# Which groups of a graph convolution are multiplied by an adjacency and which are gathered: 20 and 5, or 15 and 10, with a recorded engine order

## Chip, cores and metric

The kernel runs on one core of one Trainium2 chip. The metric is the device time of one execution in microseconds, as the median of several runs.

## The reference

Four layers, each a graph convolution and a feed-forward part, run over 3125 nodes of 256 features and 53125 edges, sorted by destination; each node has one edge to itself in that list. The change touches the third graph part (L2) and the building of what it multiplies with. Cut to what matters:

```python
def _L2_gnn_ref(x, W1, b1, W2, b2, edge_index):
    loops = jnp.arange(n)
    src = concatenate([edge_index[0], loops])      # the loops come on top of the
    dst = concatenate([edge_index[1], loops])      # own edges already in the list
    deg = segment_sum(ones, dst); dinv = rsqrt(deg)
    norm = dinv[src] * dinv[dst]
    def gcn_conv(h, W, b):
        m = (h @ W)[src] * norm[:, None]
        return segment_sum(m, dst) + b
    x1 = gcn_conv(x, W1, b1)
    x1 = x1 / max(norm_of_row(x1), 1e-12)
    x2 = gcn_conv(x1, W2, b2)
    return x2 + x

x = x + _L1_gnn_ref(...); x = x + _L1_ffn_ref(layernorm(x), ...)
x = x + _L2_gnn_ref(layernorm(x), W1, b1, W2, b2, edge_index)
x = x + _L2_ffn_ref(layernorm(x), ...)             # a switch layer; its router comes first
```

All else (the other three graph parts and feed-forward parts) is the same in both kernels.

## The kernel before

**Groups and slots.** The nodes are ranked by degree and cut into `NT` = 25 groups of 128. Group g has `KS[g]` slots, as many as its node with the most edges has: 41, 25, 23, 22, 21, 21, 20, 20, 19, 19, 18, 18, 17, 17, 16, 16, 16, 15, 15, 14, 14, 13, 12, 11, 10. `BATCH` = 5 groups share the small operations. A node lies on a partition, its features along the free axis.

**A convolution** (`edge_sum`) starts from `own`, the rows h @ W times dinv, in SBUF, and from the same rows in a table in HBM. The groups below `GD` = 20 are sums by matrix products: `products(g)` loads `adj[g]`, 0 and 1 in bf16, 128 x 3200 and 800 KB (tile `adj_g`, three buffers), and multiplies its 25 blocks with the rows. So that bf16 loses nothing, the rows are split into three bf16 parts (`F12`, in the buffer of `XNT`, and `F3_`); per block there is one matmul of 512 columns (L2851) and one of 256 (L2854). Two additions put the halves together with `own` (`sum`, L2871 and L2872). The groups from `GD` on are gathered: each slot is an indirect DMA of 128 rows, issued by POOL (`gt<-gcn,z_i`, issued in the helper at L1082), four slots to a tile `gt` of three buffers (`C4` = 4), and DVE sums a tile's slots and adds them to `own` (`g_part`, L2840 and L2841). One tile is taken beside each product (`next(beside)`). The own edge counts twice, once by the list and once by the loop.

**The order of groups** is written out: 0 to 14 by product, then 20 to 24 gathered, then 15 to 19 by product.

**Tails.** After a group's sum, `tail1` of the first convolution scales it, adds the bias and sums its squares; after each batch of five the rows are normalised, transposed by PE, copied by ACT and multiplied by the second weights (`to_table`, L2884), and a batch's rows go to the second table. `tail2` of the second convolution adds the residual; after each batch come the layer norm (`XN`, L2931), PE transposes (L1632), an ACT copy (L1633), the router matmul (L2937) and the logits `lgs` (L2938). The next stage begins with `bests`, the maximum over all logits. The tails are generators, so that a step of them follows each later group.

**Order on the engines.** Each engine takes its instructions in one order. What the program text gives is taken by a scheduler, which puts ready work of each engine first by its own costs, except inside `tc.manual_schedule(engines=...)`, where the named engines keep the order of the text. DMA issues lie on SP's queue, indirect DMAs on POOL's.

**The adjacencies** are built earlier, beside the gates of the L1 feed-forward part, one group to a step (`beside_gates`): `one_hots` (L2051, DVE) makes `em_p` and `em_b` for the edges of group g, `edge_blocks` multiplies them (`em_ps`, L2066, PE) and ACT copies the counts to `em_a` (L2073, L2077), which SP stores to `adj[g]`. `edge_columns` and `edge_places` prepare the slots of these groups.

Of the kernel before, what the change touches and what calls it, by code (L numbers as in the profile page):

```python
# [11 lines left out]
F32 = mybir.dt.float32  # L12
# [3 lines left out]
ALU = mybir.AluOpType  # L16
# [4 lines left out]
P = 128  # L21
D = 256
KD = D // P
N = 3125
NT = (N + P - 1) // P
# [16 lines left out]
def parts(tc, a, k, X, XNT):  # L42
# [387 lines left out]

    def moe(E, F, gates, w1, b1, w2, b2):

        FC = F // P
        with tc.tile_pool(name="mw", bufs=2) as mw, tc.tile_pool(name="mc", bufs=1) as mc:
# [5 lines left out]
            with tc.tile_pool(name="mps", bufs=3, space=PSUM) as mps, tc.tile_pool(name="mh", bufs=2) as mh:  # L440
# [4 lines left out]
                for e in range(E):  # L445
                    w1_sb = mw.tile([P, KD, F], F32, name="w1_sb")
                    nc.sync.dma_start(w1_sb, w1[e].rearrange("(k p) f -> p k f", p=P))
# [581 lines left out]
C4 = 4  # L1029


def profile():


    mean = (E - N) / N
    p = [math.exp(-mean)]
    for i in range(1, 200):
        p.append(p[-1] * mean / i)
    ks = []
    for g in range(NT):  # L1040
        d = 1
        while True:
            tail = max(1.0 - sum(p[:d]), 0.0)
            c = N * tail
            if (c < 1e-3) if g == 0 else (c + 4.0 * math.sqrt(c * (1.0 - tail)) <= P * g):
                break
            d += 1
        ks.append(d)
    return ks


KS = profile()
# [1 line left out]
TOT = sum(KS)  # L1054
DC = KS[0] + 3

GD = 20
BATCH = 5


# [20 lines left out]
def gather(nc, out_, table, idx):  # L1081
    return nc.gpsimd.indirect_dma_start(out=out_, out_offset=None, in_=table, in_offset=index(idx))  # L1082
# [509 lines left out]
def quick(ctx: ExitStack, tc: tile.TileContext, a: dict, out: bass.AP, k):  # L1592
# [3 lines left out]
    nc, dram, ident, ident_b, ones = tc.nc, k.dram, k.ident, k.ident_b, k.ones  # L1596
# [22 lines left out]
    def table_of(name, width, rows=NP + 1):  # L1619

        t = dram.tile([rows, width], F32, name=name)
        nc.sync.dma_start(t[NP : NP + 1, :], zero[:, :width])
        return t

    def batches():
        return [range(b, b + BATCH) for b in range(0, NT, BATCH)]
# [175 lines left out]
    def chunks(g):  # L1802
        return [(c, min(C4, KS[g] - c)) for c in range(0, KS[g], C4)]
# [157 lines left out]

    adj = dram.tile([GD, P, NT * P], BF16, name="adj")


    TILES, at = [], 0
    for g in range(GD):
        w = min(10, P // KS[g])
        n = -(-P // w)
# [4 lines left out]
    TB = -(-at // P)  # L1973
    slots_d = dram.tile([2 * P * OFF[GD]], F32, name="slots_d")

    def slots_of(g):
        return slots_d[2 * P * OFF[g] : 2 * P * OFF[g + 1]]

    t_at = q.tile([P, GD], F32, name="t_at")
    with tc.tile_pool(name="ep", bufs=1) as pool:  # L1980
        NJ = max(n for _, n, _ in TILES)
        firsts = pool.tile([P, GD, NJ], F32, name="ep_first")
        for g, (w, _, _) in enumerate(TILES):
# [3 lines left out]
        nc.gpsimd.iota(j_f, pattern=[[0, 1]], base=0, channel_multiplier=1, allow_small_or_imprecise_dtypes=True)  # L1987
        past = pool.tile([P, GD, NJ], F32, name="ep_past")
        nc.vector.tensor_scalar(past, firsts, j_f, None, op0=ALU.is_le)
# [687 lines left out]
    def beside_gates(pool, wp, psum):  # L2677


        EX, F = 4, 512  # L2680
        FC = F // P
        b1_sb = wp.tile([P, EX, FC], F32, name="x_b1")
# [4 lines left out]
        def load(e):  # L2687
            w1 = pool.tile([P, KD, F], F32, name="x_w1")
            nc.sync.dma_start(w1, a["L1_ffn_W1"][e].rearrange("(k p) f -> p k f", p=P))
            w2 = pool.tile([P, FC, D], F32, name="x_w2")  # L2690
            nc.sync.dma_start(w2, a["L1_ffn_W2"][e].rearrange("(f p) d -> p f d", p=P))
            b2 = pool.tile([P, D], F32, name="x_b2")
            nc.sync.dma_start(b2, a["L1_ffn_b2"][e : e + 1, :].to_broadcast([P, D]))
            ws[e] = w1, w2, b2
# [78 lines left out]
    with tc.tile_pool(name="ge", bufs=1) as gc, tc.tile_pool(name="gy", bufs=4) as gp:  # L2773
        gates = gc.tile([P, NT, C], F32, name="gates")
        nc.sync.dma_start(gates, gd.rearrange("(p t) w -> p t w", p=P))
        for g in range(NT):
            y = gp.tile([P, 4, D], F32, name="y")
            nc.sync.dma_start(y, each_d[:, g * P : (g + 1) * P, :].rearrange("e p d -> p e d"))
            for e in range(4):
                nc.vector.scalar_tensor_tensor(X[:, g, :], y[:, e, :], gates[:, g, e : e + 1], X[:, g, :],  # L2780
                                               op0=ALU.mult, op1=ALU.add)
# [14 lines left out]
    with tc.tile_pool(name="ng", bufs=3) as gp, tc.tile_pool(name="ns", bufs=3) as sp, \  # L2796
# [3 lines left out]
        own = wp.tile([P, NT, D], F32, name="own")  # L2800
# [6 lines left out]
        tables = [table_of(f"gcn{i}", D) for i in (1, 2)]  # L2807
# [8 lines left out]
        F12 = XNT.rearrange("p k n -> p (k n)").bitcast(BF16).rearrange("p (b s d) -> p b s d", s=2, d=D)  # L2816
        F3_ = wp.tile([P, NT, D], BF16, name="F3")

        def edge_sum(table, tail):


            for gs in batches():
                b = slice(gs[0], gs[-1] + 1)
                F = sp.tile([P, BATCH, D], F32, name="F", bufs=2)
                nc.scalar.copy(F12[:, b, 0, :], own[:, b, :])
                nc.vector.tensor_sub(F, own[:, b, :], F12[:, b, 0, :])
                nc.scalar.copy(F12[:, b, 1, :], F)
                nc.vector.tensor_sub(F3_[:, b, :], F, F12[:, b, 1, :])
            tails, ready = [], set()

            def gathered():

                for g in range(GD, NT):
                    for c, n in chunks(g):
                        t = gp.tile([P, C4, D], F32, name="gt", bufs=3)
                        for i in range(n):
                            k_ = OFF[g] - OFF[GD] + c + i
                            gather(nc, t[:, i, :], table, zi[:, k_ : k_ + 1])
                        part = sp.tile([P, D], F32, name="g_part", bufs=2)
                        nc.vector.tensor_reduce(part, t[:, :n, :].rearrange("p s d -> p d s"), AX.X, ALU.add)  # L2840
                        nc.vector.tensor_add(own[:, g, :], own[:, g, :], part)  # L2841
                        if c + n == KS[g]:
                            ready.add(g)
                        yield 0

            def products(g):
                A = gp.tile([P, NT, P], BF16, name="adj_g")
                nc.sync.dma_start(A.rearrange("p b j -> p (b j)"), adj[g])
                acc = psum.tile([P, 2, D], F32, name="acc", bufs=2)
                for b in range(NT):  # L2850
                    nc.tensor.matmul(acc.rearrange("p s d -> p (s d)"), A[:, b, :],  # L2851
                                     F12[:, b, :, :].rearrange("p s d -> p (s d)"),
                                     start=(b == 0), stop=False, skip_group_check=True)
                    nc.tensor.matmul(acc[:, 0, :], A[:, b, :], F3_[:, b, :], start=False, stop=(b == NT - 1),  # L2854
                                     skip_group_check=True)
                return acc

            beside = gathered()
            for g in [*range(GD - BATCH), *range(GD, NT), *range(GD - BATCH, GD)]:
                if g < GD:  # L2860
                    acc = products(g)
                    next(beside, None)
                while g >= GD and g not in ready:
                    next(beside)
                for t in list(tails):
                    if next(t, None) is None:
                        tails.remove(t)
                s_ = own[:, g, :]
                if g < GD:
                    s_ = sp.tile([P, D], F32, name="sum", bufs=2)  # L2870
                    nc.vector.tensor_add(s_, acc[:, 0, :], own[:, g, :])  # L2871
                    nc.vector.tensor_add(s_, s_, acc[:, 1, :])  # L2872
                t = tail(g, s_)
                if t:
                    tails.append(t)
            for t in tails:
                for _ in t:
                    pass
# [37 lines left out]
            yield 0  # L2916

        st = SimpleNamespace()
        edge_sum(tables[0], tail1)

        def tail2(g, acc):
            nc.vector.tensor_add(X[:, g, :], X[:, g, :], b2)
# [3 lines left out]
            if g % BATCH == BATCH - 1:  # L2926
# [3 lines left out]
                for i, g_ in enumerate(gs):  # L2930
# [8 lines left out]
                    if i % 2:  # L2939
                        yield 0  # L2940
                nc.sync.dma_start(sw_xn[gs[0] * P : (gs[-1] + 1) * P, :].rearrange("(t p) d -> p t d", p=P),
                                  XN[:, gs[0] : gs[-1] + 1, :])

        edge_sum(tables[1], tail2)


    with tc.tile_pool(name="wc", bufs=1) as wc, tc.tile_pool(name="ww", bufs=6) as ww, \
# [82 lines left out]
    with tc.tile_pool(name="ag", bufs=abufs) as gp, tc.tile_pool(name="am", bufs=2) as mp, \  # L3030
# [28 lines left out]
        for o in range(0, TOT, 160):  # L3059
            n = min(160, TOT - o)  # L3060
# [321 lines left out]
```

## Time and profile before

| | |
|---|---|
| median of 6 runs | 5787.91 us (5776.34 to 5796.77) |
| the profiled execution | 5784.42 us, its span 5782.7 us |
| mean granted TensorE clock | 0.753 |
| busy: PE, DVE, ACT, POOL | 3383.1, 3113.0, 1217.1, 2833.4 us |
| L2 convolutions: first gather, second one's first gather, `bests` | 3817.4, 4073.2, 4311.8 us from the span's start |
| gathers in them | 3817.4 to 3869.3 (39), 3879.0 to 3905.2 (21); 4073.2 to 4122.4 (39), 4132.5 to 4159 (21) |
| first and last `sum` of each | 3838.9 and 4053.1; 4083.6 and 4298.5 us |

The span is that of one execution taken by the hardware profiler. "Busy" is the time in which an engine works on an instruction; idle time is put down to what ended it, a DMA, another engine's result, or "issue", where the profile shows nothing that the engine waited for. PEld are weight loads, which may overlap the matmuls. A group of instructions is named by its line, its engine, its operation and its tiles, then the count, the busy time and the mean of one in ns. Line numbers of helpers (L1082, L1632) stand for all their callers, so that the tiles tell the stages apart.

### The profile page before, as it was taken

Reading aid. Unit: us, or ns where it says so; the run is one execution under the profiler, and the core shown is the slowest. Engines: PE = TensorE matmul, PEld = TensorE weight load, DVE = VectorE, ACT = ScalarE, POOL = GpSimd, SP = SyncE. Lnnn points to the kernel's source line nnn. Section 1 sums busy time; section 2 is a strip of 40 time slices with the busy share of each in tenths; the row PEclk is TensorE's granted clock in tenths of the full one; section 3 lists DMA queues with packets and bytes.
Section 4 is the critical chain, followed back from the end, with each engine's and each line's share of the span. In section 5 each row is a group of like instructions: output and inputs, shape, how many; then the busy total and the mean of one; then the engine's idle time right before and its main releaser. Section 6 shows DMA issues by size and latency. Waiting matters only on the chain. (4 is left out here: it accounts for less than half of the span.)

```text
span 5782.7 us, 44145 instructions
## 1 busy us (share of the span) xinstructions
PE 3383.1 (59%) x13157; PEld 2313.3 (40%) x13157; DVE 3113.0 (54%) x6119; ACT 1217.1 (21%) x3115; POOL 2833.4 (49%) x3011
## 2 busy tenths in 40 slices
PE   4245554355487964445337565059679355556995
PEld 3234443233354533334124343036354233334885
DVE  5377887798685754561124331463441567886002
ACT  1222323455531200000113231121112101111221
POOL 1567673577765036676644445430403466661223
PEclk7677777677798976676568777579885677787998
DMA  3534442334321233332212221353324333332664
GB/s 104 132 101 114 110 124 79 81 100 113 99 29 48 113 94 92 88 89 76 28 43 70 51 63 24 82 144 102 120 79 123 95 87 93 94 89 73 195 195 153
DMA packets 321843, 548.13 MB, mean 95 GB/s; under 512 B 100906, under 2 KB 224028, under 8 KB 318254
## 3 DMA queue, kind: packets, MB, share of 16 engines
q0 software_dynamic: 121840, 290.47, 20.7%
q1 hardware_dynamic: 186757, 244.81, 13.1%
q10 hardware_dynamic: 12982, 9.77, 0.6%
q8 instruction: 112, 1.84, 0.1%
q14 instruction: 152, 1.25, 0.1%
HBM read 429.05 MB, written 118.80 MB: 95 GB/s over the span
## 5 line engine op out<-in xcount | busy, mean ns | idle before, releaser
L1082 POOL DMA_INDIRECT gt<-T,recs x856 | 907.4, 1060 | 443.0 <-issue 344.7
L1841 PE MATMUL acc<-wv,ident 128*128 128x256 f32 x1812 | 557.6, 462 | 285.9 <-issue 153.0
L1082 POOL DMA_INDIRECT gt<-rel,relz x428 | 414.1, 968 | 433.2 <-issue 368.3
L1082 POOL DMA_INDIRECT gt<-gm,recs x428 | 405.6, 948 | 403.1 <-issue 200.3
L1841 PEld LDWEIGHTS acc<-wv,ident 128*128 128x128 f32 x1812 | 412.7, 235 | 408.2 <-issue 174.0
L1082 POOL DMA_INDIRECT gt<-TA,recs x428 | 436.9, 1021 | 254.8 <-issue 125.9
L1841 PE MATMUL acc<-gt,wv 128*128 128x256 f32 x906 | 296.0, 486 | 310.3 <-DVE wv L1852 256.0
L2851 PE MATMUL acc<-XNT,adj_g 128*128 128x512 bf16 x1000 | 347.4, 394 | 50.7 <-issue 39.6
L2702 PE MATMUL x_ps<-XNT,x_w 128*128 128x512 f32 (+1 forms) x448 | 244.7, 679 | 222.6 <-ACT x_h L2704 138.8
L1954 PE MATMUL acc<-gt,ident 128*128 128x256 f32 x856 | 281.4, 467 | 145.3 <-issue 121.1
L1841 PEld LDWEIGHTS acc<-gt,wv 128*128 128x128 f32 x906 | 210.3, 243 | 389.7 <-DVE wv L1852 194.4
L2723 DVE TENSOR_TENSOR x_y<-x_o,x_b 128x512 f32<-128x512 f32 (+1 forms) x52 | 34.4, 670 | 612.9 <-remote 245.4
L1914 ACT ACTIVATE m<-m 128x1024 f32<-128x1024 f32 (+3 forms) x246 | 243.1, 988 | 492.6 <-DVE m L1911 306.8
L1911 DVE TENSOR_TENSOR m<-gt,R 128x1040 f32<-128x1040 f32 (+6 forms) x246 | 281.5, 1144 | 93.8 <-DMA gt<-T,recs 54.5
L2854 PE MATMUL acc<-F,adj_g 128*128 128x256 bf16 x1000 | 280.7, 281 | 36.7 <-issue 28.4
L1919 DVE TENSOR_TENSOR m<-m,fixed 128x1040 f32<-128x1040 f32 (+6 forms) x246 | 280.2, 1139 | 36.3 <-ACT m L1914 27.1
L1954 PEld LDWEIGHTS acc<-gt,ident 128*128 128x128 f32 x856 | 193.0, 233 | 220.6 <-issue 152.6
L1082 POOL DMA_INDIRECT gt<-gcn,z_i x120 | 117.2, 977 | 320.6 <-DMA gcn<-own 168.0
L2716 PE MATMUL x_o<-x_w,x_h 128*128 128x256 f32 x800 | 208.2, 404 | 48.4 <-issue 48.1
L2702 PEld LDWEIGHTS x_ps<-XNT,x_w 128*128 128x128 f32 x448 | 92.5, 232 | 317.3 <-issue 167.7
L3142 PE MATMUL e_ps<-EW,att 128*128 128x512 bf16 (+4 forms) x233 | 94.5, 481 | 191.7 <-ACT att L3125 73.6
L3273 PE MATMUL fh_ps<-xt,w 128*128 128x256 f32 x896 | 200.0, 382 | 0.8 <-DVE xt L3265 0.8
(665 smaller groups left out, 7162.9 us busy)
## 6 DMA issues: line engine op xcount, KB each, us to landing
w<-in_L_ffn_W_dram SPq DMA_DIRECT2D x56, 1024.0 KB
adj_g<-adj SPq DMA_DIRECT2D x40, 800.0 KB
rel<-hx SPq DMA_DIRECT2D x25, 1024.0 KB
adj<-em_a SPq DMA_DIRECT2D x20, 800.0 KB
gt<-T,recs POOLq DMA_INDIRECT x856
y<-each_d SPq DMA_DIRECT2D x25, 512.0 KB
each_d<-x_y SPq DMA_DIRECT2D x24, 512.0 KB
gt<-rel,relz POOLq DMA_INDIRECT x428
```

The lines of the kernel that those rows point to most:

```text
L1082: return nc.gpsimd.indirect_dma_start(out=out_, out_offset=None, in_=table, in_offset=index(idx))
L1841: nc.tensor.matmul(acc, w, v, start=(c + s == 0 and bias is None), stop=(c + s == K - 1))
L1911: nc.vector.tensor_add(m[:, :n, :], st[g].tiles[c][:, :n, :W], st[g].R[1][:, None, :].to_broadcast([P, n, W]))
L1914: nc.scalar.activation(v, v, AF.Abs)
L1919: nc.vector.tensor_mul(m[:, :n, :], m[:, :n, :], att_row[:, None, :].to_broadcast([P, n, W]))
L1954: nc.tensor.matmul(accs[g], ident, t[:, s, :], start=False, stop=(last and s == n - 1))
L2702: nc.tensor.matmul(ps[:, :n], ws[e][0][:, c, f_ * P : (f_ + 1) * P], XNT[:, c, c0 : c0 + n], start=(c == 0), stop=(c == KD - 1))
L2716: nc.tensor.matmul(ps[:, j, :], ht[:, f_, (i + j) * P : (i + j + 1) * P], ws[e][1][:, f_, :], start=(f_ == 0), stop=(f_ == FC - 1))
L2851: nc.tensor.matmul(acc.rearrange("p s d -> p (s d)"), A[:, b, :], F12[:, b, :, :].rearrange("p s d -> p (s d)"), start=(b == 0), stop=Fals ...
L2854: nc.tensor.matmul(acc[:, 0, :], A[:, b, :], F3_[:, b, :], start=False, stop=(b == NT - 1), skip_group_check=True)
L3142: nc.tensor.matmul(e_ps[:, :z, :].rearrange("p s d -> p (s d)"), att, EW[: att.shape[0], s : s + z, :].rearrange("p s d -> p (s d)"), star ...
L3273: nc.tensor.matmul(ps[:, i, :], ld[j][1][:, c, (f_ + i) * P : (f_ + i + 1) * P], xt[j][:, c, :], start=(c == 0), stop=(c == KD - 1))
```

## The change

`GD` falls from 20 to 15: groups 15 to 19 are gathered too, so that five adjacencies fewer are built, stored and loaded, and each convolution has 15 products. The own edge is no longer gathered: the chunks cover `KS[g]` - 1 slots, and the first addition of a group takes 2 times `own`. A convolution has 126 gathers in 36 tiles (60 in 17 before). Two tiles are taken beside each of the first ten products and three beside each of the last five. The groups go 0 to 9 by product, 15 to 19 gathered, 10 to 14 by product, 20 to 24 gathered. The splitting into bf16 parts is staggered by one batch, and both calls of `edge_sum` record the order of PE, ACT and DVE. POOL and SP are still ordered by the scheduler.

```diff
-GD = 20
+GD = 15
 BATCH = 5
...
         def edge_sum(table, tail):
-            for gs in batches():
-                b = slice(gs[0], gs[-1] + 1)
-                F = sp.tile([P, BATCH, D], F32, name="F", bufs=2)
-                nc.scalar.copy(F12[:, b, 0, :], own[:, b, :])
-                nc.vector.tensor_sub(F, own[:, b, :], F12[:, b, 0, :])
-                nc.scalar.copy(F12[:, b, 1, :], F)
-                nc.vector.tensor_sub(F3_[:, b, :], F, F12[:, b, 1, :])
+            bs = [slice(gs[0], gs[-1] + 1) for gs in batches()]
+            Fs = []
+            for i in range(len(bs) + 1):
+                if i < len(bs):
+                    F = sp.tile([P, BATCH, D], F32, name="F", bufs=2)
+                    nc.scalar.copy(F12[:, bs[i], 0, :], own[:, bs[i], :])
+                    nc.vector.tensor_sub(F, own[:, bs[i], :], F12[:, bs[i], 0, :])
+                    Fs.append(F)
+                if i:
+                    nc.scalar.copy(F12[:, bs[i - 1], 1, :], Fs[i - 1])
+                    nc.vector.tensor_sub(F3_[:, bs[i - 1], :], Fs[i - 1], F12[:, bs[i - 1], 1, :])
...
                 for g in range(GD, NT):
-                    for c, n in chunks(g):
+                    for c in range(0, KS[g] - 1, C4):
+                        n = min(C4, KS[g] - 1 - c)
                         t = gp.tile([P, C4, D], F32, name="gt", bufs=3)
...
-                        nc.vector.tensor_add(own[:, g, :], own[:, g, :], part)
-                        if c + n == KS[g]:
+                        nc.vector.scalar_tensor_tensor(own[:, g, :], own[:, g, :], 2.0 if c == 0 else 1.0, part,
+                                                       op0=ALU.mult, op1=ALU.add)
+                        if c + n == KS[g] - 1:
                             ready.add(g)
...
             beside = gathered()
-            for g in [*range(GD - BATCH), *range(GD, NT), *range(GD - BATCH, GD)]:
+            early = NT - BATCH
+            for g in [*range(GD - BATCH), *range(GD, early), *range(GD - BATCH, GD), *range(early, NT)]:
                 if g < GD:
                     acc = products(g)
-                    next(beside, None)
+                    for _ in range(2 if g < GD - BATCH else 3):
+                        next(beside, None)
...
-        edge_sum(tables[0], tail1)
+        ET = mybir.EngineType
+        with tc.manual_schedule(engines={ET.PE, ET.Activation, ET.DVE}):
+            edge_sum(tables[0], tail1)
...
-        edge_sum(tables[1], tail2)
+        with tc.manual_schedule(engines={ET.PE, ET.Activation, ET.DVE}):
+            edge_sum(tables[1], tail2)
```

## The prediction

> **What bounds the kernel now.** I read the page first, for the groups of the graph convolution, then the lines view and the busy time by windows of that stage, then the timeline of one stretch, and last the lines view of the gate stage, where the adjacencies are built. The page's rows:
>
> ```profile
> L2851 PE MATMUL acc<-XNT,adj_g 128*128 128x512 bf16 x1000 | 347.4, 394 | 50.7 <-issue 39.6
> ...
> L2854 PE MATMUL acc<-F,adj_g 128*128 128x256 bf16 x1000 | 280.7, 281 | 36.7 <-issue 28.4
> ...
> L1082 POOL DMA_INDIRECT gt<-gcn,z_i x120 | 117.2, 977 | 320.6 <-DMA gcn<-own 168.0
> ```
>
> Both convolutions lie between 3817.4 us (first gather) and 4311.8 us (`bests`): 255.8 us to the second one's first gather at 4073.2, then 238.6, together 494.4. The sums of the products (L2871) leave the rhythm of the stage: every 9.2 us once no gather runs, which is 8.1 us for the 25 pairs of matmuls and about 1.05 us for one node's table or router work. PE looks like the bound. The windows say more; their columns are busy us (and instructions) of PE, weight loads, DVE, ACT and POOL, the granted clock, the DMA share and GB/s:
>
> ```profile
> 3820.00:3900.00 80.00, 42.80 (x204) 21.35 (x202) 39.10 (x57) 1.26 (x1) 52.74 (x55) 0.77 0.46 130
> 3980.00:4060.00 80.00, 79.35 (x474) 51.21 (x472) 36.03 (x88) 19.82 (x39) 0.00 (x0) 1.00 0.31 105
> 4080.00:4160.00 80.00, 40.01 (x178) 18.64 (x175) 38.47 (x55) 0.00 (x0) 52.84 (x55) 0.70 0.46 132
> 4160.00:4240.00 80.00, 78.19 (x480) 48.18 (x481) 28.46 (x93) 3.44 (x11) 0.00 (x0) 0.96 0.33 111
> ```
>
> While POOL gathers, PE gets through 204 and 178 matmuls in 80 us; without gathers, 474 and 480. The timeline shows that this is not a wait for data (start, duration, idle time before and its releaser):
>
> ```profile
> 3858.33 0.95 POOL L1082 DMA_INDIRECT gt<-gcn,z_i  x1 [0.30 <-issue]
> 3859.11 0.11 PEld L2854 LDWEIGHTS <-adj_g 128*128 128x128 bf16 x1 [2.71 <-issue]
> 3859.58 0.95 POOL L1082 DMA_INDIRECT gt<-gcn,z_i  x1 [0.30 <-issue]
> 3859.81 0.37 PE L2854 MATMUL acc<-F,adj_g 128*128 128x256 bf16 x1 [1.52 <-issue]
> 3860.84 0.95 POOL L1082 DMA_INDIRECT gt<-gcn,z_i  x1 [0.30 <-issue]
> 3861.21 0.10 PEld L2851 LDWEIGHTS <-adj_g 128*128 128x128 bf16 x1 [2.00 <-issue]
> ```
>
> PE takes one instruction in 0.7 to 1.4 us, with "issue" before it, while POOL issues a gather every 1.25 us (0.95 and 0.30). This starved state begins some 15 us after PE and POOL have both been busy, and ends 2 to 4 us after POOL stops. In the first convolution it fills 3847 to 3871 and 3892.5 to 3908.7, in the second 4100 to 4126 and 4147 to 4162: 81 us in all, 0.54 of the 120 x 1.255 = 151 us of gathering. That is the row on which everything turns, since the change doubles the gathers.
>
> The stage now closes as a sum, to 2 us. First convolution: 13.4 (first gather to first product) + 20 x 8.1 + 20 x 1.05 + 40 starved + 20.1 (last sum at 4053.1 to the next gather) = 257 against 255.8. Second: 2.3 + 162 + 20 x 0.9 + 41 + 13.3 (4298.5 to 4311.8) = 237 against 238.6.
>
> **Products removed.** Five of 20 in each convolution, 10 x 8.1 = -81 us, and the table work no longer between products, 10 nodes x 1.0 = -10, which returns in the tails below. Ten adjacency loads leave SP's queue too; each lands 4 to 5 us after its issue beside a product of 8.1, so they were hidden, and the new place of groups 15 to 19 costs nothing for the same reason.
>
> **Gathers added.** Own rows no longer gathered, each group takes KS-1: 126 instead of 60 per convolution, 132 more in all, x 1.255 = 166 us more on POOL, whose queue holds little else in this stage. Gathering takes 158 us per convolution beside 148 us of PE work, so it can't hide in a part of it: the two must overlap fully to gain. The price on PE is the starved share. By the share of before, 0.54 x 158 = 85 us per convolution, 170 against 81: +89. Bounds: if POOL always paused within 15 us of PE work (three gt tiles are 12 gathers, 15.1 us), nothing is starved, -81; if it ran through, 158 - 15 + 3 = 146 per convolution, +211. I take the share, since POOL is ahead or paused as three tiles and DVE allow, which is also so in before.
>
> The page "Runtime: NRT & Kernel Launch" of the Trainium skill (Instruction fetch mechanics) says that a queue refills ahead in blocks of 256 instructions and that this is mostly hidden: by it the stage would have no starved time, and this term would be -81 instead of +89. The rows above speak against that for PE beside gathers, and the measured share decides.
>
> **Recorded order.** PE, ACT and DVE now run as the program is written. Two things stand in line that the scheduler had moved apart. On DVE the `sum` of a product is queued behind the reductions of two or three gathered tiles, and the PE's transposes of a tail behind a DVE scale that stands there too:
>
> ```profile
> L2840 DVE TENSOR_REDUCE g_part<-gt 128x256 f32<-128x1024 f32 (+3 forms) x34 | 54.8, 1615 | 48.7 <-DMA gt<-gcn,z_i 46.1 <-issue 2.6
> ```
>
> The row shows that these reductions wait for the gathered rows. In the second convolution a node's tail (XN, transposes, ACT copy, router matmul, `lgs`) is a chain of 2.2 to 2.5 us; beside a product PE gave 0.9 to it, so in line each costs about 1.4 more: 15 nodes x 1.4 = +21. In the first a step between the halves lets them overlap: 15 x 0.4 = +6. Waits of `sum` for landing tiles: 0 to 60 us (the last five products have 12 gathers, 15.1 us, beside 9 us of PE, 10 x 6 = 60); much of that is the starved time again, so I take +15. Against this stands what a better order could save; below nothing I see only the 10 us gap between the two runs of gathers.
>
> **The ends.** Groups 10 to 14 and 20 to 24 now both have their tails after the last product: five nodes more at about 2 us in the first convolution, +10, and a batch of 5 at 2.5 and its statistics in the second, +14. The doubling of the own row is a factor in an existing addition, and the 38 extra reductions and additions (1.6 and 0.42 us) are 77 us of DVE work in a stage where DVE is busy 36 to 49% of the windows: their cover is that idle time, and without it they would be +77. The F splits change only order: 0.
>
> **The gate stage.** Five adjacencies fewer are built:
>
> ```profile
> L2051 DVE TENSOR_TENSOR em_b<-places,em_cols 128x3200 bf16<-128x3200 f32 (+11 forms) x20 | 71.1, 3557 | 0.0
> ...
> L2051 DVE TENSOR_TENSOR em_p<-places,em_cols 128x2048 bf16<-128x2048 f32 (+11 forms) x20 | 59.6, 2979 | 19.5 <-PE x_ps L2702 9.5 <-issue 8.4 <-PE em_ps L2066 1.6
> ```
> ```profile
> L2066 PE MATMUL em_ps<-em_b,em_p 123*128 123x75 bf16 (+11 forms) x424 | 60.7, 245 | 127.9 <-issue 123.7 <-ACT em_a L2077 4.1
> ```
>
> DVE loses 5 x 6.5 = 33 us, PE 79 of 424 matmuls, 11 us, ACT some 41 casts at 0.5, 20 us. No engine is full there (PE 70, 49 and 69% in 3160 to 3450, DVE 26 to 38%, POOL 37 to 54%), and each waits for the others, so between 0 and 33 + 11 = 44 us come off; I take the middle, -22.
>
> **Sum.** -81 - 10 + 89 + 21 + 6 + 15 + 10 + 14 - 22 = +42 us on an execution of 5784.4, whose span is 5782.7: 5826. That execution was 3.5 us below the median of the six runs, 5787.9; against the median it is 5830.
>
> **Rivals.** *No starving (faster).* The three gt tiles hold POOL to bursts of 12 gathers, 15 us, inside what PE runs at full speed, and the ordered DVE releases tiles only as PE delivers its products. Then gathering sets the pace: 158 + 2 to land + 30 (or 27) at the end, 377 for both, with the 42 us of waits in line 419 against 494: -75, with the gate stage -97, 5691; with half of the starving gone, about 5760. It decides once the starved time of both convolutions falls under 170 - 42 = 128 us, 0.41 of the gathering. For it: the state ends within 4 us of a pause. Against: POOL starts again as soon as PE moves, and 8 gathers (10 us) per product exceed the product's 8.1. Chance 0.30.
>
> *One long run (much slower).* DVE is free enough to release each tile at once, and POOL runs through: +122 on the forecast, 5952. The windows with 55 gathers in 80 us are the nearest rows, and there POOL had its pauses. Chance 0.06.
>
> *The two cancel.* The starved time at 116 to 140 us, a share of 0.37 to 0.44: within 12 us. Chance 0.08. My forecast, slower, with a share between 0.44 and about 0.75: 0.56.
>
> **Numbers.** The measurement tells 0.2%, 12 us, from no change. The outer rivals stand at 5691 and 5952; a share of 0.32 with the gate stage at -44 gives 5830 - 69 - 22 = 5739, a share of 0.70 with the gate stage at 0 gives 5830 + 51 + 22 = 5903; the range is 5735 to 5905. The forecast's own range is 5800 to 5905. Slower: 0.56 + 0.06 = 0.62; same 0.08; faster 0.30.
>
> **What would show it.** In the changed kernel 252 rows of gt<-gcn at a pitch of 1.25 us, and PE windows with some 180 to 200 matmuls in 80 us beside them for most of both convolutions: right. PE with over 300 matmuls in such windows, POOL waiting for `g_part` L2840 after every 12 gathers, and the stage under 480 us: the faster rival. `lgs` at 2.2 to 2.5 us steps between products shows the waits in line. The gate stage should end 0 to 44 us earlier against its own start; more than that makes the sum wrong there.

## The result

The changed kernel is slower, by less than half a per cent: 5813.7 us median (21 runs) against 5788.1 (47 runs), a ratio of 1.0048 (1.0037 to 1.0059). The profiled execution took 5805.4 us with a span of 5803.7.

Against the profile before, three stretches moved. The gate stage, from its first `gm` gather to the first `gcn` gather, took 1030.3 us (1046.6 before). The two convolutions took 257.1 (3780.3 to 4037.4) and 291.6 us (to `bests` at 4329.0), 548.7 in all against 494.4: +54.3. Everything ahead of the gate stage ended 20.7 us earlier although its code is the same; runs of one kernel differ by as much (5753 to 5810 for the kernel before), so sums are made here stage by stage: the two stages that the change touches moved by -16 and +54 us, +38 together.

The page's rows of the stage after, in the form of those shown for before (idle time and what ended most of it stand behind the last bar):

```profile
L1082 POOL DMA_INDIRECT gt<-gcn,z_i x252 | 247.2, 981 | 342.2 <-DVE g_part L2845 131.1
...
L2857 PE MATMUL acc<-XNT,adj_g 128*128 128x512 bf16 x750 | 280.7, 417 | 40.8 <-issue 33.5
...
L2860 PE MATMUL acc<-F,adj_g 128*128 128x256 bf16 x750 | 219.9, 293 | 34.8 <-issue 27.1
```

There are 252 gathers, as computed, but POOL was held for 131 us by `g_part`, a tile not yet given back. And PE's "issue" idle in front of the product matmuls, which is the starved state as the profile puts a number to it, did not double: 33.5 + 27.1 = 60.6 us against 39.6 + 28.4 = 68.0 before. The windows agree (same columns as before):

```profile
3800.00:3880.00 80.00, 52.66 (x266) 26.83 (x265) 37.84 (x62) 0.59 (x2) 46.27 (x48) 0.79 0.44 133
3880.00:3960.00 80.00, 68.02 (x344) 41.22 (x342) 48.46 (x91) 8.34 (x22) 42.78 (x44) 0.86 0.47 147
4050.00:4130.00 80.00, 51.96 (x253) 26.05 (x251) 39.90 (x62) 0.00 (x0) 49.17 (x51) 0.83 0.46 137
4130.00:4210.00 80.00, 58.22 (x296) 35.18 (x297) 45.35 (x106) 4.26 (x12) 30.46 (x31) 0.77 0.36 116
4210.00:4290.00 80.00, 41.63 (x202) 23.87 (x200) 43.12 (x92) 2.72 (x8) 33.79 (x35) 0.73 0.30 78
```

In the first four windows PE gets through 253 to 344 matmuls beside 31 to 51 gathers, more than the 204 and 178 beside 55 gathers of before; the worst window is the last, 202 matmuls beside 31 gathers. What keeps PE idle there is told by its waits in the two convolutions (engine, line, what it waited for: us in total, times, longest). Before:

```profile
PE acc L2851 <- issue: 39.6, 25, 4.8
PE acc L2854 <- issue: 28.4, 16, 2.4
...
PE tps L1632 <- DVE XN L2931: 5.7, 2, 5.1
...
PE tps L1632 <- DVE h L2909: 0.6, 1, 0.6
PE c_ps L2884 <- ACT ht L1633: 0.6, 1, 0.6
PE c_ps L2937 <- ACT ht L1633: 0.5, 1, 0.5
```

After:

```profile
PE tps L1632 <- DVE XN L2941: 40.0, 17, 10.7
...
PE c_ps L2947 <- ACT ht L1633: 26.0, 24, 7.6
PE tps L1632 <- DVE ln_r L78: 14.3, 2, 9.4
PE c_ps L2892 <- ACT ht L1633: 7.9, 11, 2.0
...
PE tps L1632 <- DVE h L2917: 6.4, 3, 2.4
```

These tail inputs cost PE 7.4 us before and 94.6 after: +87. The busy time of PE over both convolutions, before and after, and below it that of the product matmuls alone (same columns; without POOL in the last two):

```profile
3817.40:4311.80 494.40, 399.27 (x2270) 238.65 (x2267) 206.01 (x470) 44.10 (x98) 119.44 (x126) 0.88 0.34 107
3780.30:4329.00 548.70, 368.58 (x1789) 211.22 (x1786) 294.08 (x562) 47.36 (x99) 249.41 (x258) 0.78 0.37 113
```
```profile
3817.40:4311.80 494.40, 357.00 (x1970) 0.00 (x0) 33.70 (x80) 0.00 (x0) 0.88 0.34 107
3780.30:4329.00 548.70, 291.81 (x1489) 0.00 (x0) 25.23 (x60) 0.00 (x0) 0.78 0.37 113
```

The stage's balance on PE is then complete. Its busy time fell by 31 us: that of the products by 65, while the time in which matmuls of the tails run with no product beside them rose from 42.3 to 76.8 us, +34, though there are 300 of them in both kernels. Its idle time rose from 95.1 to 180.1 us, +85: waits for tail inputs +87, starving -7, all other idle time +5. Together that is +54. One node's tail, from the end of the stage, shows how such a wait looks (start, duration, idle time before and its releaser):

```profile
4326.49 0.66 PE L1632 MATMUL tps<-ident,XN 128*128 128x128 f32 x2 [0.70 <-DVE XN L2941]
4327.25 0.38 ACT L1633 ACTIVATE ht<-tps 128x256 f32<-128x256 f32 x1 [2.57 <-PE tps L1632]
...
4327.69 1.06 PE L2947 MATMUL c_ps<-rws,ht 128*128 128x32 f32 x4 [0.53 <-ACT ht L1633]
4328.79 0.19 DVE L2948 TENSOR_TENSOR lgs<-c_ps,rbs 128x32 f32<-128x32 f32 x1 [2.44 <-PE c_ps L2947]
```

XN, transposes, copy, router matmul and `lgs` follow each other, and the previous `lgs` stands at 4325.84: 2.95 us for a node, in which PE works 1.7 us.

### The profile page after: what moved, and what is told of

It is laid out like the page before. It is cut to its first block, busy times and chain, and to the rows that moved or that the text cites. A ratio compares the mean times of both kernels' runs of the same rounds, so it can differ in the third digit from the quotient of the medians.

```text
span 5803.7 us, 43166 instructions
## 1 busy us (share of the span) xinstructions
PE 3364.2 (58%) x12576; PEld 2298.0 (40%) x12576; DVE 3164.3 (55%) x6160; ACT 1203.3 (21%) x3073; POOL 2963.6 (51%) x3138
## 3 DMA queue, kind: packets, MB, share of 16 engines
q14 instruction: 154, 1.25, 0.1%
## 4 chain that ended last, share of the span: by engine, by line
DVE 24%; issue 24%; PE 22%; POOL 12%; another core or an unknown queue 9%; DMA 5%; ACT 3%; DVEq 0%; ACTq 0%; POOLq 0%; SPq 0%
POOL gt L1082 7%; DVE m L1911 3%; DVE m L1919 3%; PE hx_ps L112 3%; PE x_ps L2702 3%; POOL rp_g L1082 3%; DVE wv L1858 3%; PE x_o L2716 2%; PE acc L2857 2%; PE acc L1841 2%; PE acc L1954 1%; DVE m L3163 1%; PE acc L2860 1%; DVE L L1924 1%
## 5 line engine op out<-in xcount | busy, mean ns | idle before, releaser
L1841 PE MATMUL acc<-wv,ident 128*128 128x256 f32 x1812 | 571.0, 472 | 291.8 <-issue 176.3
L1082 POOL DMA_INDIRECT gt<-gcn,z_i x252 | 247.2, 981 | 342.2 <-DVE g_part L2845 131.1
L2857 PE MATMUL acc<-XNT,adj_g 128*128 128x512 bf16 x750 | 280.7, 417 | 40.8 <-issue 33.5
L1919 DVE TENSOR_TENSOR m<-m,fixed 128x1040 f32<-128x1040 f32 (+6 forms) x246 | 280.2, 1139 | 25.9 <-issue 11.2
L2860 PE MATMUL acc<-F,adj_g 128*128 128x256 bf16 x750 | 219.9, 293 | 34.8 <-issue 27.1
L1086 POOL DMA_INDIRECT top_out<-ys,into x56 | 56.6, 1011 | 279.7 <-DVE ys L3299 262.3
```

The costliest lines, as they stand in the source:

```text
L1841: nc.tensor.matmul(acc, w, v, start=(c + s == 0 and bias is None), stop=(c + s == K - 1))
L1919: nc.vector.tensor_mul(m[:, :n, :], m[:, :n, :], att_row[:, None, :].to_broadcast([P, n, W]))
```

## The experiments

Theory A: the recorded order costs the time, because tails stand in PE's line and wait for their inputs. Theory B: the additional gathers cost it, because POOL's gathering starves PE. Times differ much between the sets of runs, so every ratio is against the kernel before in its own set. In the sets of the first traces and of experiments 1 to 4 and 10 to 12 before took 5771 to 5789 us; in those of experiments 5 to 9 it took 5103 to 5105. The text calls them the slow and the fast condition. Why there are two is not settled. It is not a fixed property of a chip, as one of the expectations has it: by the record's numbers chip 4 gave 5105 us in the set of experiments 5 to 8 and 5789 us in that of experiment 12. "Starved" below is PE's idle time put down to "issue" in front of the product matmuls, "tail waits" are those for XN, ln_r, h and ht as listed above. The expectations count starved time more widely (87, 170, 75 and 140 us where the table has 68.0, 132.7, 56.6 and 89.2).

| kernel | ratio to before | convolutions | starved | tail waits |
|---|---|---|---|---|
| before | | 494.4 us | 68.0 | 7.4 |
| the changed kernel | 1.0048 | 548.7 | 60.6 | 94.6 |
| 1: 15 products, scheduler | 1.0057 (1.0035 to 1.0079) | 538.1 | 132.7 | 25.9 |
| 2: 20 products, recorded | 1.0044 (1.0029 to 1.0059) | 520.4 | 41.9 | 51.9 |
| 3: 20 products, scheduler | 0.9981 (0.9962 to 0.9999) | 480.6 | 56.6 | 5.7 |
| 4: changed, other steps | 0.9995 (0.9977 to 1.0012) | 510.2 | 89.2 | 33.6 |

**1. Ten gathered groups without the recorded order.**

```diff
-        with tc.manual_schedule(engines={ET.PE, ET.Activation, ET.DVE}):
-            edge_sum(tables[0], tail1)
+        edge_sum(tables[0], tail1)
```

and the same for the second convolution.

> The changed kernel without the recorded order: fifteen products, ten gathered groups, own edges from SBUF, but PE, ACT and DVE ordered by the scheduler. The two convolutions took 549 us in the changed kernel (257 and 292) and 494 before. Theory A, waits in line: the recorded order costs the 53 us of the second convolution, because its tails stand in PE's line; the convolutions fall to about 490 to 510 and the kernel to 5760 to 5780. Theory B, starving: the 132 more gathers cost PE more than the ten products saved, whatever the order; the convolutions stay at 540 to 590 and the kernel at 5805 to 5850.

Measured: 1.0057, convolutions 270.1 and 268.0 us. Theory A said 490 to 510, theory B 540 to 590: B, within 2 us of its lower end. PE's waits in the stage:

```profile
PE acc L2857 <- issue: 73.1, 48, 3.2
PE acc L2860 <- issue: 59.6, 38, 2.9
...
PE c_ps L2945 <- ACT ht L1633: 16.8, 2, 10.7
```

Starving doubles, 132.7 against 68.0 (twice the gathers), and the tail waits are small. In this order the prediction's main term is what happens. The 16.8 us for `ht` belong to it too, as experiment 11 shows.

**2. The recorded order with five gathered groups**: `GD = 20` in the changed kernel.

> The changed kernel with 20 products and five gathered groups again (own edges from SBUF, recorded order kept). Theory A: the recorded order alone costs 30 to 60 us, the convolutions take 525 to 555 us, the kernel 5820 to 5850. Theory B: 110 gathers in place of 252 starve PE for about 60 us as in the kernel before, the convolutions take 480 to 495, the kernel 5775 to 5790.

Measured: 1.0044, 520.4 us: between the two theories, nearer to A. Against experiment 3 the recorded order alone costs 40 us in the convolutions. Its tail waits are 46 us more, its starving 15 less, and PE's busy time is 18 us more (415.9 against 397.5), mostly tail matmuls without a product beside them.

**3. Neither**: `GD = 20` and no recorded order; what is left of the change is the own edge from SBUF, the order of the groups and the staggered split.

> 20 products, scheduler's order, own edges from SBUF: the change with neither the ten gathered groups nor the recorded order. Both theories: ten gathers fewer than before, the convolutions 480 to 495, the kernel 5775 to 5790. It gives the base for the other three.

Measured: 0.9981, 480.6 us, as expected, and the fastest of this set. So each half of the change loses by itself, 40 us for the recorded order (2 against 3) and 58 for the ten groups (1 against 3), and the two together lose 68 rather than 98. For the whole kernel, by the ratios, these losses are 36, 44 and 39 us, since ten gathered groups also save 18 us in the gate stage.

**4. The changed kernel with other steps in its tails.**

```diff
+            for i in range(BATCH):
+                nc.vector.tensor_scalar(hs[i], hs[i], r[:, i : i + 1], None, op0=ALU.mult)
             yield 0
             for i, g_ in enumerate(gs):
-                nc.vector.tensor_scalar(hs[i], hs[i], r[:, i : i + 1], None, op0=ALU.mult)
...
+                for pair in (gs[0:2], gs[2:4], gs[4:5]):
+                    hts = []
+                    for g_ in pair:
+                        ht = sp.tile([P, KD, P], F32, name="ht", bufs=4)
+                        to_columns(sp, psum, XN[:, g_, :], ht)
+                        hts.append((g_, ht))
+                    routed()
+                    turned = hts
+                    yield 0
```

`routed` holds the router matmuls and `lgs` of the pair before, and `ht` has four buffers.

> The changed kernel with its tails cut into other steps: the five scales of a batch at once in a step of their own, and in the second convolution the transposes of two nodes one step ahead of their router matmuls, so that PE finds each input ready when the recorded order comes to it. Theory A: 35 to 50 us come back, the convolutions take 500 to 515 us, the kernel 5765 to 5780. Theory B: the starving remains, at most 10 us come back, the kernel 5800 to 5815.

Measured: 0.9995, 510.2 us. Theory A's numbers, -38.5 us in the convolutions. The tail waits fall from 94.6 to 33.6, and about half comes back as starving, 60.6 to 89.2. PE's waits here:

```profile
PE acc L2857 <- issue: 54.3, 45, 3.2
PE acc L2860 <- issue: 34.9, 40, 1.7
PE tps L1632 <- DVE XN L2942: 24.7, 3, 9.1
```

**5. Plain loads in place of the gathers**, in the scheduler's order of experiment 1.

```diff
-                            gather(nc, t[:, i, :], table, zi[:, k_ : k_ + 1])
+                            r_ = k_ % NT * P
+                            nc.sync.dma_start(t[:, i, :], table[r_ : r_ + P, :])
```

> The kernel with 15 products in the scheduler's order (538 us for the two convolutions, 170 of them starved), with each indirect gather of 128 rows replaced by a plain load of 128 consecutive rows on SP's queue: as many bytes and as many transfers, none issued by POOL. The rows are not those of the edges, so the gathered groups' sums are others. Theory B1, POOL's issuing of gathers starves PE: the starved time falls from 170 to under 20 us and the convolutions take 340 to 420 us, the kernel 5620 to 5710. Theory B2, the transfers themselves do (their bytes or their number): 120 to 180 us stay starved and the convolutions take 500 us or more.

Measured: 4984.4 us, ratio 0.9763, beside a kernel before of 5104.7. The convolutions took 373.9 us from the first load to `bests`, with no "issue" idle time of PE. But the fast condition made the expectation's absolute times void, and the next three traces showed that gathers starve nothing in it; the test was repeated as experiment 12.

**6 and 7. One and two gt tiles in experiment 3** (`bufs=1`, `bufs=2` for `gt`).

> 20 products, scheduler's order, own edges from SBUF (481 us for the convolutions, 75 starved, 5774 us in all), with one gt tile in place of three, so that POOL issues four gathers and then pauses until they have landed and DVE has reduced them, some 4 us. If starving needs gathers without a pause and ends 2 to 4 us after one: starved time under 20 us, the convolutions 420 to 450 us, the kernel 5715 to 5745. If it is set by the number of gathers alone: 75 us stay, the convolutions 475 to 500 us, the kernel 5770 to 5790.

> The same with two gt tiles: while one is reduced, the other is filled, so that POOL's pauses are short or none. If a pause of 2 to 4 us is what ends the starving: 50 to 75 us stay starved, the convolutions 465 to 485 us, the kernel 5760 to 5780. If the number of gathers alone sets it: as with three.

Measured: 1.0089 (1.0074 to 1.0105) and 0.9986 (0.9977 to 0.9995); convolutions 507.4 and 457.8 us. In neither trace is PE idle on "issue" before a product matmul, with two tiles as little as with one, so the question about pauses isn't answered. With one tile PE waits 87.0 us for `sum`, with two 53.7.

**8. Two tiles in experiment 4**: `bufs=2` for `gt`.

> The changed kernel with the other steps of the tails (510 us, 140 starved, 5780 us in all), with two gt tiles in place of three. Each sum that DVE waits for now stops POOL four gathers earlier. If pauses of POOL cure starving: 90 to 120 us starved, the convolutions 485 to 505 us, the kernel 5755 to 5775. If gathering sets the pace of this version: the convolutions 515 to 540 us, the kernel 5785 to 5810.

Measured: 0.9985 (0.9976 to 0.9994), convolutions 456.4 us, starved 0, tail waits 49.4. Also here the condition, not the tile count, took the starving away, as experiment 9 shows with three tiles.

**9. The changed kernel again.**

> The changed kernel itself once more, beside the kernel before. The set of runs with plain loads and with one and two tiles came from another chip, on which the kernel before took 5105 us instead of 5783 to 5788 and on which none of the three traces with gathers has more than 22 us of starved time. On a chip where before takes about 5785 us, both theories expect the changed kernel at 5805 to 5825 us, 20 to 35 us over before, with 80 to 100 us starved. On a chip where before takes about 5105 us: theory A, waits in line cost time whether PE starves or not, and without starving there is nothing in which they hide: the convolutions 455 to 490 us, the kernel between 15 us faster and 20 us slower than before. Theory B, gathers lose only by starving: the ten products fewer are kept as a gain, the convolutions 400 to 440 us, the kernel 30 to 60 us faster than before.

It came in the fast condition: 5117.0 us against 5102.7, ratio 1.0027 (1.0016 to 1.0037). Convolutions 217.9 and 259.2, 477.1 us in all; 1.5 us starved, tail waits 107.1. A window of it, beside gathers:

```profile
3290.00:3370.00 80.00, 65.91 (x374) 38.62 (x382) 51.68 (x80) 1.42 (x5) 61.10 (x63) 0.94 0.57 176
```

374 matmuls beside 63 gathers, where the kernel before had 204 beside 55 in the slow condition. Without starving the change still loses, as theory A expects; theory B's 30 to 60 us of gain did not appear. No trace of before was taken in this condition; the nearest, experiment 7, has 457.8 us for the convolutions. Experiment 8, with other steps in its tails and two tiles, has 58 us less of tail waits and convolutions 21 us shorter.

**10 and 11. Before and experiment 1 again.** They came in the slow condition.

> The kernel before, for its trace on the chip of this set. If it takes about 5105 us here, the starved time should be under 20 us (87 in the first trace), the convolutions 455 to 470 us (494), and the gate stage, from its first gm gather to the first gcn gather, 740 to 750 us (1046). If it takes about 5785 us, all three as in the first trace.

> 15 products in the scheduler's order, which starved PE for 170 us and took 538 us for the convolutions where before took 5783. On a chip where before takes about 5105 us, theory B (gathers lose only by starving): the convolutions 380 to 430 us and the kernel 30 to 75 us faster than before, ratio 0.985 to 0.994. Theory A alone (whatever stands in line): 455 us or more and no gain. On a chip where before takes about 5785 us it repeats 1.0057.

Before repeats its trace (493.7 us, 76.5 starved), experiment 1 gives 1.0061 (1.0040 to 1.0082) with 539.8 us and 110.5 starved; two traces of one kernel agree to 2 us in the convolutions. Its tail waits are 43.8 us, 37.6 of them two waits for `ht`. The longer one shows that starving is not PE's alone (timeline; the rows left out are gathers):

```profile
4241.34 0.47 DVE L2932 SCALAR_TENSOR_TENSOR X<-own,dinv_r,X 128x256 f32<-128x256 f32 x1
...
4248.07 0.95 POOL L1082 DMA_INDIRECT gt<-gcn,z_i  x1 [0.31 <-issue]
4253.48 0.32 SPq L2854 DMA_DIRECT2D adj_g<-adj  x1
4253.49 0.42 DVE L2879 TENSOR_TENSOR sum<-acc,own 128x256 f32<-128x256 f32 x1 [11.67 <-remote]
4253.59 0.38 ACT L1633 ACTIVATE ht<-tps 128x256 f32<-128x256 f32 x1 [38.84 <-remote]
4254.03 0.42 PE L2945 MATMUL c_ps<-rws,ht 128*128 128x32 f32 x1 [27.68 <-ACT ht L1633]
```

PE's transposes for this `ht` had ended at 4223.5, yet ACT copied them 30 us later. From 4241.8 to 4253.5 no engine but POOL runs anything, and 4.5 us after POOL's last gather SP, DVE and ACT start within 0.1 us. What released them the profile can't place ("remote"). The trace of experiment 1 has the same at its two waits for `ht`, so starving cost PE 132.7 + 16.8 = 149.5 us there and 110.5 + 37.6 = 148.1 here. In the changed kernel two of the waits for `ht`, 7.6 and 6.4 us, are of this kind. DVE's and ACT's idle time put down to "remote" in this stage is 17.9 and 0 us in before, 45.6 and 56.9 in the changed kernel, and none in any of the four traces with gathers in the fast condition.

The scheduler's order with 15 products was therefore not seen in the fast condition, and whether it would gain there stays open.

**12. Plain loads in the slow condition.**

> 15 products in the scheduler's order with plain loads of 128 consecutive rows from SP's queue in place of the indirect gathers (other rows than those of the edges). On the chip of the first plain run, where before took 5105 us, it took 4984 and its trace stood against no starving. On a chip where before takes about 5785 us and gathering starves PE: theory B1, POOL's issuing of gathers starves PE: starved time under 20 us, the two convolutions 370 to 400 us (538 with gathers), the kernel 5620 to 5680. Theory B2, the transfers themselves do it: 120 us or more starved, the convolutions 500 us or more. On a chip where before takes about 5105 us it repeats 4984.

Measured: 5611.1 us, ratio 0.9697 (0.9660 to 0.9735) beside a before of 5789.4. The convolutions took 370.8 us (538 and 540 with gathers), and PE is never idle on "issue" before a product matmul. As many bytes in as many transfers, issued by SP, starve nothing: theory B1, with the kernel 9 us under its range. The edit changes the issuing engine and the kind of transfer together, so it does not tell which of the two starves. Without gathers the condition makes hardly a difference to this stage, 370.8 us here and 373.9 in experiment 5. The 167 us are more than the starved time. The trace has two reasons at hand, whose shares were not measured: the loads are issued every 0.48 us (median) where gathers come every 1.25, and the first one at 3764.3, while the table is still being stored (last store issued at 3794.1).

## Why the prediction was right, and where only in its sum

The forecast was +42 us; the medians moved by 26, the traces by 21, and the two stages concerned by 38. Sign and size held, but three terms of the sum did not.

- **Gathers, +89 for the starved share: wrong in the recorded order, about right without it.** The step took the share of before because POOL would be "ahead or paused as three tiles and DVE allow, which is also so in before". In the recorded order it isn't so: a tile is given back by a reduction that stands in DVE's line behind sums and tails, POOL waited 131 us for that, and PE's starving changed by -7 us, or +7 with the two starved waits for `ht`. In the scheduler's order, with those waits, it came to +82 and +72 (149.5 and 148.1, against 68.0 and 76.5).
- **Waits in line and the ends, 21 + 6 + 15 + 10 + 14 = +66: too small.** Tail waits alone rose by 87, 14 of them starving. A node's chain measured 2.95 us rather than 2.2 to 2.5, and the XN scale and `ln_r` waited for DVE besides. On top, tail matmuls that had run beside products now ran alone, +34, where the sum took 10 off for table work. The mechanism of the waits was the right one: other steps took 61 us of them away.
- **Products, -81: too large.** The products' busy time fell by 65 us, not by 81. Five products of 20 went in each convolution, but PE ran the rest at a lower granted clock, 0.83 and 0.74 in the two convolutions against 0.90 and 0.87; a matmul of 512 columns took 417 ns against 394.
- **Gate stage, -22: right in the slow condition.** Four traces with 15 adjacencies took 1023 to 1033 us, four with 20 took 1044 to 1047: -18. In the fast condition the stage took 743 to 748 us with either, so nothing is saved there.

The errors cancelled: +64 was forecast for the convolutions, +54 measured. They are not independent, as the four kernels of experiments 1 to 3 and the changed one show. Starving and waiting in line are two ways for PE to lose the same time. The likely reason, of which the traces show POOL's waits for `g_part`, is that while PE waits in line DVE waits behind it, POOL stops, and the starved state ends. Experiment 4 shows the exchange from the other side: 61 us of waits taken away, 29 us of starving back. Nothing in the prediction foresaw this exchange, so that the sum came out within 10 us was luck. Its signs say the same. The 180 to 200 matmuls beside gathers showed in one window of five; POOL's waits for `g_part` and over 300 matmuls, signs of the faster rival, showed too (344, in one window), in a kernel that was slower.

The rivals: "no starving" was half true. Its condition, under 128 us starved, held in the first set of runs (60.6) and in the fast condition (1.5), yet the kernel was slower both times, by 26 and 14 us. The convolutions took 548.7 and 477.1 us, not 419, so its price of 42 us for the waits was the part that failed: tail waits were 94.6 and 107.1. "One long run" did not occur: POOL's waits for `g_part` forbid it.

The page "Runtime: NRT & Kernel Launch" of the Trainium skill (Instruction fetch mechanics) was cited for refills of an instruction queue that are mostly hidden. In the slow condition PE takes one instruction in 0.7 to 1.4 us beside indirect gathers, with nothing else that the profile shows; in the fast condition it does not. The trace of before also holds the packets of the instruction queues. Those of 16 KB took 0.9 to 1.4 us each in the convolutions, and none lies in the four starved stretches; three of 8 KB do, of 0.5 to 1.0 us. That speaks against a long refill under way there. Whether something else holds up the fetching, these runs do not tell.

## What to carry to other kernels

A recorded order must be cut so that each engine finds its input ready: issue the producing step one step earlier than the consuming one, over a stretch of other work; here that was worth 31 us by the ratios to before. Look at what ends the idle time on the bounding engine before and after, and expect two causes of idle time to replace each other: taking one away pays only partly. A wait for another engine can be that engine's starving: look whether its input had long been there. And a saving in products on the busiest engine can be worth less than its instructions: here their busy time fell by 65 us of 357, less than the quarter that went, while the granted clock fell, and matmuls that had run beside them came to stand alone.

## What the runs showed of the hardware

- The same kernel took 5771 to 5789 us in some sets of runs and 5103 to 5105 in others, with both on one chip. In the stage studied the traces differ where POOL gathers: in the one condition PE falls to one instruction in 0.7 to 1.4 us, in the other it runs on. With plain loads the stage took 370.8 and 373.9 us in the two. The gate stage, which gathers too, took 1044 to 1047 against 743 to 745 us (20 adjacencies). What sets the condition is open.
- Where it occurs, it hangs on POOL's indirect gathers and not on the bytes: plain loads of as many bytes from SP's queue left PE with no "issue" idle time in the same stage (132.7 and 110.5 us with gathers). It holds DVE, ACT and SP too: ACT copied a finished transpose 30 us late, 4.6 us after POOL's last gather.
- PE's granted clock is low where PE often idles, by waits in line or by starving: 0.74 in the second convolution of the changed kernel, 0.76 in the fast condition, 0.74 in experiment 1, against 1.00 in a window of products alone.
